# Per-row statistics of the quantised weights, and the removal of the rounding constant together with the zero point, issued on GpSimd instead of VectorE

## The chip, the cores and the metric

The kernel runs on one core of one Trainium2 chip. The metric is device time in microseconds of one execution. The kernel before took 2467.56, 2470.31 and 2482.42 us in three runs; the median is 2470.31 us. In the profile's rows PE is TensorE (matrix products), PEld its weight loads, DVE is VectorE, ACT is ScalarE, POOL is GpSimd, SP is the engine that issues most transfers. The clock is the share of full speed that the throttle granted TensorE.

## What is computed

Four layers follow one another on `x`, two sequences of 1024 tokens with 288 channels, with `ctx`, two sequences of 154 tokens, as context. Attention has 16 heads of 18 channels. Layers 0 and 1 are quantised blocks, layers 2 and 3 plain attention from `x` to `ctx`, whose keys are taken as two sets (86 and 68), each with a softmax of its own. What the change concerns is the quantised product in layers 0 and 1:

```python
def quant_linear(q, s, qsum, w, b):
    wmax = jnp.max(w, axis=1)
    wmin = jnp.min(w, axis=1)
    sw = (wmax - wmin) / 255.0 + 1e-08
    zw = _ste_round(-wmin / sw) - 128.0
    qw = jnp.clip(_ste_round(w / sw[:, None]) + zw[:, None], -128.0, 127.0)
    acc = jnp.einsum('bnk,ok->bno', q, qw) - qsum * zw
    return acc * (s * sw) + b
...
h = layer_norm(x, ln1_g, ln1_b, 1e-06)
q8, s, sm = quant_act(h)
q = quant_linear(q8, s, sm, wq1, bq1).reshape(b, n, H, D)
k = quant_linear(q8, s, sm, wk1, bk1).reshape(b, n, H, D)
v = quant_linear(q8, s, sm, wv1, bv1).reshape(b, n, H, D)
a = attn(q, k, v)
a8, sa, sma = quant_act(a)
x = x + quant_linear(a8, sa, sma, wo1, bo1)
...
h = quant_linear(q8, s, sm, wfc1, bfc1)
```

After the self-attention come a cross-attention to `ctx` with a mask (`wq2` and `wo2` quantised, `wk2` and `wv2` not) and a feed-forward 288 to 1152 to 288 with a gelu (`wfc1`, `wfc2` quantised). `_ste_round` rounds to the nearest integer, ties to even.

## The kernel before

**Weights.** Every quantised weight is loaded, quantised row by row with its output channels on the partitions, transposed on TensorE and kept. `quantise_rows` (from L218) does the quantising. It is called by `prep` (L305: wv1, wo1, wo2 and four blocks of 288 rows of wfc1, on 96 partitions in three slices of 288), by `prep_T` (L322: wk1, wq1, wq2, on 108 partitions in three slices of 288) and by `prep_fc2` (L337: wfc2 in three blocks of 96 rows, each one slice of 1152). A layer has 13 such weights, layers 0 and 1 together 26.

**One weight.** The steps of `quantise_rows`, all on VectorE unless another engine is named: L225 and L226 take the maximum and minimum of each row (three per partition, or one for wfc2). L227 and L228 make the scale `sw`, L229 its reciprocal `rs`, L231 and L232 the largest magnitude in units of the scale, L233 the rounding constant `mg` (the constant whose addition rounds a float to an integer, or 0 where the values are so large that nothing is to be rounded), L234 to L237 the zero point `zw`. Then, for each slice of 288 or 1152, L240 multiplies by `rs` and adds `mg`, which rounds, and L243 takes `mg` off again and adds `zw`. L248, on GpSimd, clips the whole weight from both sides and writes it as bf16. GpSimd then makes the twelve extra columns that carry zero point and bias through the product (L253 to L261, with the helper `three`, L210 to L216, which splits a number into three parts). The transposes on TensorE wait for the clipped weight and these columns.

**Buffers.** The float weight stands in a tile of pool `big` (three buffers), the clipped one in `bf` (three), the statistics in `wstat` (two).

**Order.** Every engine works its own queue in order. A planner with a time model (L57, `tc.block(schedule_with_timeline_sim=True)`) sets the order in the queues, so that instructions of several stages are interleaved. The main line is the self-attention: for each of two layers and two sequences it makes logits on TensorE twice, once with the queries on the partitions (L600), whose rows VectorE reduces to their maxima (L607, 1024 instructions), and once the other way (L660), whose exponentials ScalarE makes (L662); L674 multiplies them by the values. The logits go through three banks of PSUM (pool `ps_s`, L68), which both kinds share. `beside` (L1623) feeds pieces of a side line between the pieces of the main one. The prologue prepares layer 0's wk1, wq1 and wv1 (`prepare_first`, from L997). Then stand, beside the four self-attentions: layer 0's wo1 and the second sequence's queries and keys, wq2 and wo2, fc1 and fc2; then the rest of layer 0's block for the first sequence, with layer 1's wk1, wq1, wv1; then layer 1's wo1 and the rest for the second sequence, with layer 1's wq2 and wo2; last layer 1's fc1 and fc2. Layers 2 and 3 follow without quantised weights.

**Other work on GpSimd** that the prediction names: the mask's addition to the logits of the cross-attention (L641), the layer norm's power (L414, small; L416 on VectorE takes it up) and its gain and offset (L430), additions to the residual (L472), the splitting of queries and keys into bf16 parts (L510, L517), and the transfers issued there (L178, L200, L1402). L646 on VectorE takes the maxima of the cross-attention's logits after L641.

Of the kernel before, what the change touches and what calls it, by code (L numbers as in the profile page):

```python
# [13 lines left out]
ALU = mybir.AluOpType  # L14
# [3 lines left out]
B, S, C, T = 2, 1024, 288, 154  # L18
# [13 lines left out]
MAGIC = 12582912.0  # L32
# [12 lines left out]
NZ = 12  # L45
# [8 lines left out]
def tile_xattn(ctx: ExitStack, tc: tile.TileContext, ins: dict, out: bass.AP):  # L54
    nc = tc.nc
# [86 lines left out]
    def bf(name):  # L142
        return work.tile([P, 3 * HQ], BF16, tag="bf", name=name, bufs=3)
# [71 lines left out]
        eng.tensor_tensor(r, r, high, ALU.subtract)  # L215
        eng.tensor_tensor(low, r, middle, ALU.subtract)  # L216

    def quantise_rows(w, bias, n, width, pad, name):  # L218

        rows = w.shape[0]
        wm = small.tile([rows, 10, 3], F32, tag="wstat", name=name, bufs=2)
        mx, mn, sw, rs, am, mg, u, zw, z, be = (wm[:, j, 0:n] for j in range(10))
        nc.vector.tensor_reduce(mx, w, AX.X, ALU.max)  # L225
        nc.vector.tensor_reduce(mn, w, AX.X, ALU.min)  # L226
        nc.vector.tensor_tensor(sw, mx, mn, ALU.subtract)  # L227
        nc.vector.tensor_scalar(sw, sw, 1.0 / 255.0, 1e-8, ALU.mult, ALU.add)  # L228
        nc.vector.reciprocal(rs, sw)  # L229

        nc.vector.scalar_tensor_tensor(am, mn, -1.0, mx, ALU.mult, ALU.max)  # L231
        nc.vector.tensor_tensor(am, am, rs, ALU.mult)  # L232
        nc.vector.tensor_scalar(mg, am, 4194304.0, MAGIC, ALU.is_lt, ALU.mult)  # L233
        nc.vector.tensor_tensor(u, mn, rs, ALU.mult)  # L234
        nc.vector.scalar_tensor_tensor(u, u, -1.0, mg, ALU.mult, ALU.add)
        nc.vector.tensor_tensor(u, u, mg, ALU.subtract)
        nc.vector.tensor_scalar(zw, u, 128.0, None, ALU.subtract)  # L237
        for j in range(n):
            c = slice(j, j + 1)
            nc.vector.tensor_scalar(  # L240
                w[:, j, :], w[:, j, :], rs[:, c], mg[:, c], ALU.mult, ALU.add
            )
            nc.vector.tensor_scalar(  # L243
                w[:, j, :], w[:, j, :], mg[:, c], zw[:, c], ALU.subtract, ALU.add
            )
        q = bf(f"{name}q")
        qv = view(q[:rows, 0 : n * (width + pad)], n=n, i=width + pad)
        nc.gpsimd.tensor_scalar(qv[:, :, 0:width], w, 127.0, -128.0, ALU.min, ALU.max)  # L248

        def col(k):  # L250
            return qv[:, :, width + k]

        nc.gpsimd.tensor_copy(z, zw)  # L253
        three(nc.gpsimd, [col(2 * k) for k in range(3)], z)
        nc.gpsimd.tensor_copy(
            qv[:, :, width + 1 : width + 6 : 2], qv[:, :, width : width + 6 : 2]
        )
        nc.gpsimd.tensor_tensor(be, bias, rs, ALU.mult)
        three(nc.gpsimd, [col(6), col(7), col(9)], be)
        for k, src in ((8, 6), (10, 7), (11, 6)):  # L260
            nc.gpsimd.tensor_copy(col(k), col(src))  # L261
        if pad > NZ:
            nc.gpsimd.memset(qv[:, :, width + NZ :], 0.0)
        return qv, sw
# [54 lines left out]
        scale_row(row, [sw[:, n : n + 1] for n in range(3)], name)  # L319
        return qw, row  # L320

    def prep_T(W, w_name, b_name, scaled=False, queue=nc.sync, bias=None):  # L322


        name = w_name
        col = W.tile([FR, 3], F32, "col", f"{name}col")
        if bias is None:
            bias = bias_cols(b_name, [(f, f + FR) for f in FT], f"{name}b")
        wv = view(big(f"{name}w")[:FR, 0 : 3 * C], n=3, i=C)
        for n, f in enumerate(FT):  # L330
            queue.dma_start(out=wv[:, n, :], in_=ins[w_name][f : f + FR, :])
        qv, sw = quantise_rows(wv, bias, 3, C, NZ, f"{name}s")
        qw = transpose_weight(W, qv, FR, name)
        nc.vector.tensor_scalar(col, sw, SCALE if scaled else 1.0, None, ALU.mult)
        return qw, col
# [618 lines left out]
    class SelfAttention:  # L954
# [42 lines left out]
        def prepare_first(self):  # L997

            w, b, name = self.w, self.b, self.name
            self.begin()
            w["ln"] = load_ln(WA, L0, 1)
            scales, qs = [], []

            def tile():
                t = query_tile(f"{name}f", "qTb")
                return t.rearrange("p j t -> p (j t)")[:, 0 : 3 * HQ]

            def normalise(hf):  # L1010
                h = apool.tile([P, HC, C], F32, tag="a", name=f"{name}h", bufs=2)
                s = small.tile([P, HC], F32, tag="st", name=f"{name}st")
                c0 = b * 8 + hf * HC
                q = ln_quantise(
                    c0, w["ln"], 1e-6, s, f"{name}l", h, tile(), nc.vector
                )
                scales.append(s)
                qs.append(q)

            def linear(hf, part, rows):  # L1020
                return linear_T(
                    qTs[hf], w[part], sbs[hf], rows[hf], f"{name}{part}", nc.vector
                )

            def scale_tile():
                return work.tile([P, HQ], F32, tag="e", name=f"{name}sb", bufs=8)[:FR]

            names = [(f"{L0}w{part}1", f"{L0}b{part}1") for part in "kqv"]
            biases = [
                bias_cols(col, [(f, f + FR) for f in FT], f"{col}t", nc.scalar)  # L1030
                for _, col in names[:2]
            ]
            load_tokens(0, 2 * HC)
            normalise(0)
            w["k"] = prep_T(WA, *names[0], queue=nc.scalar, bias=biases[0])
            qTs = [transposed(qs[0], f"{name}t", tile())]
            sbs = [token_scales(scales[0], f"{name}sb", scale_tile())]
            normalise(1)
            w["q"] = prep_T(WA, *names[1], scaled=True, queue=nc.scalar, bias=biases[1])
            made = [linear(0, "k", self.k), linear(0, "q", self.q)]  # L1040
            for m in made:
                next(m)
            qTs.append(transposed(qs[1], f"{name}t", tile()))
            sbs.append(token_scales(scales[1], f"{name}sb", scale_tile()))
            made.append(linear(1, "k", self.k))
            next(made[2])

            def others():
                for k in (0, 2, 1):
                    for put in made[k]:  # L1050
                        yield 2
                last_tokens.append(load_tokens(2 * HC, NCH, put))
                w["v"] = prep(WA, *names[2])
                yield 8
                for hf in range(2):
                    self.values(hf, qTs[hf], scales[hf])
                    yield 3
                for put in linear(1, "q", self.q):
                    yield 2

            return others()
# [587 lines left out]
    with tc.tile_pool(name="apool", bufs=1) as apool:  # L1649
        WA, WO = Weights(tpool, 1, 3, 1), Weights(apool, 1, 1, 1)  # L1650
# [97 lines left out]
```

## Time and profile before

The profiled execution spans 2474.0 us from its first to its last instruction; the runs took 2467.56 to 2482.42 us. Its mean granted clock is 0.866.

| stretch (us) | what runs in it | PE | VectorE | ScalarE | GpSimd | clock |
|---|---|---|---|---|---|---|
| 160-220 | attention of layer 0, no weight begins | 56.59 of 60 | 55.82 | 44.13 | 23.57 | 1.00 |
| 220-345 | fc1 and fc2 of layer 0, seven weights | 115.84 of 125 | 118.66 | 85.00 | 37.91 | 0.97 |
| 560-660 | layer 1's wk1, wv1, wq1 | 80.05 of 100 | 90.36 | 50.77 | 30.53 | 0.85 |
| 1240-1480 | fc1 and fc2 of layer 1, seven weights | 184.10 of 240 | 166.94 | 133.51 | 106.30 | 0.79 |

The columns are busy microseconds of each engine in a stretch. Busy time says how full an engine is there, not that others wait for it; a stretch in which one engine is full and the rest are not is paced by that engine. A row of the trace that begins with a time gives start and length of an instruction, then engine, line, operation, what is written and read, the shape, and how many instructions the row stands for. A group's row gives the least, median and largest duration in ns.

The weights start (first L225) at 21.9, 26.1, 44.5, 46.4, 122.4, 145.8 us, then, in layer 0's feed-forward, at 222.3, 253.2, 275.5, 280.7, 303.6, 310.7 and 323.3. Those of layer 1 start at 560.1, 562.0, 642.8, about 775, 1039.3, 1042.2, 1247.6, 1250.1, 1359.6, 1366.1, 1387.3, 1392.4 and 1399.7.

### The profile page before, as it was taken

The numbers are of one execution on the slowest core, as the hardware profiler recorded it, in microseconds if no ns is written. First come the engines' busy times: TensorE is split into PE (matmuls) and PEld (weight loads), VectorE is DVE, ScalarE is ACT, GpSimd is POOL, SyncE is SP. The second block draws the span as 40 slices with busy tenths as digits, with TensorE's granted clock in tenths as the row PEclk, the third lists the DMA queues.
The fourth block names the chain that finished last, engine by engine and source line by source line (L and its number), as shares of the span: only waits on it lengthen the run. The fifth ranks groups of instructions, "written<-read, shape, count | busy, mean of one in ns | idle before, by whom it ended". The sixth has DMA issues, their size and how long they took to land. (4 is left out here: it accounts for less than half of the span.)

```text
span 2474.0 us, 33572 instructions
## 1 busy us (share of the span) xinstructions
PE 1950.8 (79%) x10524; PEld 847.7 (34%) x10524; DVE 1772.7 (72%) x4213; ACT 1476.1 (60%) x2897; POOL 972.2 (39%) x2038
## 2 busy tenths in 40 slices
PE   2579988788776878887679668887778886788887
PEld 1223333332233243323333233333334343443443
DVE  6699987699775658997559848893345686656665
ACT  3257767676477667756766257756646564554443
POOL 4334224651325455532353545523157462423210
PEclk9689999899787979998889589986877888889998
DMA  3523212221001322110032031100122311212221
GB/s 75 168 66 100 68 35 69 70 64 33 13 7 47 113 71 64 44 29 14 6 100 85 23 86 43 46 9 12 31 76 87 89 48 28 55 51 81 81 66 37
DMA packets 160003, 141.58 MB, mean 57 GB/s; under 512 B 44123, under 2 KB 156339, under 8 KB 159760
## 3 DMA queue, kind: packets, MB, share of 16 engines
q1 hardware_dynamic: 148656, 121.90, 17.0%
q0 software_dynamic: 3584, 12.04, 2.0%
q10 hardware_dynamic: 7584, 5.47, 1.2%
q8 instruction: 84, 1.38, 0.2%
q14 instruction: 95, 0.78, 0.1%
HBM read 96.60 MB, written 39.37 MB: 55 GB/s over the span
## 5 line engine op out<-in xcount | busy, mean ns | idle before, releaser
L662 ACT ACTIVATE L_xattn_aatse<-L_xattn_aats 128x512 f32<-128x512 f32 x1024 | 576.3, 597 | 277.1 <-PE L_xattn_aats L660 267.2
L607 DVE TENSOR_REDUCE L_xattn_amxh<-L_xattn_amx 128x1 f32<-128x512 f32 x1024 | 658.4, 679 | 74.5 <-PE L_xattn_amx L600 71.9
L660 PE MATMUL L_xattn_aats<-L_xattn_aqT,kT 120*128 120x512 bf16 x1024 | 392.2, 409 | 88.0 <-ACT L_xattn_aatse L662 46.2
L600 PE MATMUL L_xattn_amx<-kT,L_xattn_aqT 108*128 108x512 bf16 x1024 | 387.9, 414 | 65.1 <-DVE L_xattn_amxh L607 39.5
L674 PE MATMUL L_xattn_aato<-L_xattn_aatse,L_xattn_av 128*32 128x512 f32 x2048 | 300.9, 660 | 43.7 <-ACT L_xattn_aatse L662 40.6
L641 POOL TENSOR_TENSOR L_xattn_bmxm<-L_xattn_bmxm,L_xattn_bm 128x308 f32<-128x308 f32 x256 | 200.0, 787 | 158.4 <-ACT L_xattn_bmxm L640 150.4
L660 PEld LDWEIGHTS <-kT 120*128 120x128 bf16 x1024 | 96.7, 101 | 336.2 <-issue 298.7
L662 ACT ACTIVATE L_xattn_atse<-L_xattn_ats 86x512 f32<-86x512 f32 (+1 forms) x256 | 142.7, 590 | 95.0 <-PE L_xattn_ats L660 82.2
L600 PEld LDWEIGHTS <-L_xattn_aqT 108*128 108x128 bf16 x1024 | 102.7, 103 | 216.7 <-issue 162.5
L646 DVE TENSOR_REDUCE L_xattn_mxn<-L_xattn_mx 128x2 f32<-128x172 f32 (+1 forms) x512 | 124.8, 303 | 30.7 <-PE L_xattn_mx L630 27.4
L640 ACT COPY L_xattn_bmxm<-L_xattn_bmx 128x308 f32<-128x308 f32 x256 | 104.1, 417 | 67.9 <-PE L_xattn_bmx L630 23.7
L646 DVE TENSOR_REDUCE L_xattn_bmxn<-L_xattn_bmxm 128x2 f32<-128x308 f32 x256 | 116.8, 461 | 30.6 <-POOL L_xattn_bmxm L641 30.3
L660 PE MATMUL L_xattn_ats<-L_xattn_qT,L_xattn_kT 120*86 120x512 bf16 (+1 forms) x256 | 99.7, 422 | 40.8 <-DMA L_xattn_qT<-L_xattn_mxsr 18.6
L746 DVE TENSOR_TENSOR L_xattn_batse<-L_xattn_bats,L_xattn_bmT 128x512 f32<-128x512 f32 x160 | 107.5, 680 | 25.7 <-PE L_xattn_bats L752 7.5
L747 ACT ACTIVATE L_xattn_batse<-L_xattn_batse 128x512 f32<-128x512 f32 x160 | 100.3, 631 | 40.6 <-DVE L_xattn_batse L746 36.4
L1494 PE MATMUL L_xattn_o<-wo,L_xattn_p 128*128 128x288 f32 x320 | 99.9, 451 | 5.5 <-DVE L_xattn_p L819 4.6
L674 PEld LDWEIGHTS L_xattn_aato<-L_xattn_aatse,L_xattn_av 128*32 128x32 f32 x2048 | 42.2, 112 | 173.2 <-ACT L_xattn_aatse L662 144.1
L847 DVE STREAM_TRANSPOSE L_xattn_atT<-L_xattn_ato 128x512 f32<-128x512 f32 x64 | 45.6, 713 | 61.6 <-PE L_xattn_ato L674 50.1
L630 PE MATMUL L_xattn_mx<-L_xattn_kT,L_xattn_qT 108*128 108x154 bf16 x512 | 68.9, 250 | 24.1 <-DMA L_xattn_qT<-L_xattn_r 10.4
L630 PE MATMUL L_xattn_bmx<-L_xattn_bkT,L_xattn_bqT 108*128 108x154 bf16 x512 | 72.0, 244 | 16.1 <-ACT L_xattn_bmxm L640 7.1
L1360 PE MATMUL L_xattn_co<-L_xattn_wfc2t,L_xattn_cgT 117*128 117x288 bf16 x320 | 62.4, 346 | 23.4 <-ACT L_xattn_cgT L1357 22.4
L674 PE MATMUL L_xattn_ato<-L_xattn_atse,L_xattn_v 68*32 68x512 f32 (+1 forms) x512 | 74.9, 649 | 6.7 <-ACT L_xattn_atse L662 5.8
(632 smaller groups left out, 3782.0 us busy)
## 6 DMA issues: line engine op xcount, KB each, us to landing
kT<-L_xattn_akr SPq DMA_DIRECT2D x192, 72.0 KB
L_xattn_aqT<-L_xattn_aqr SPq DMA_DIRECT2D x192, 72.0 KB
L_xattn_bqT<-L_xattn_bqr SPq DMA_DIRECT2D x192, 72.0 KB
L_xattn_qT<-L_xattn_r SPq DMA_DIRECT2D x192, 72.0 KB
L_xattn_akr<-L_xattn_akst SPq DMA_DIRECT2D x16, 324.0 KB
L_xattn_aqr<-L_xattn_aqst SPq DMA_DIRECT2D x16, 324.0 KB
L_xattn_bqr<-L_xattn_bqst SPq DMA_DIRECT2D x16, 324.0 KB
L_xattn_r<-L_xattn_qst SPq DMA_DIRECT2D x16, 324.0 KB
```

Of the source, the lines that this page charges most:

```text
L600: nc.tensor.matmul(sp, lhsT=qt[:KR, j, c * P : (c + 1) * P], rhs=kt[:KR, j, a * 512 : (a + 1) * 512], start=True, stop=True,)
L607: nc.vector.tensor_reduce(halves[:, a, c, j, :], sp, AX.X, ALU.max, negate=True)
L630: nc.tensor.matmul(sp[:, j * T : (j + 1) * T], lhsT=qt[:KR, 2 * a + j, c * P : (c + 1) * P], rhs=kt[:KR, 4 * g + 2 * a + j, 0:T], start=Tr ...
L640: nc.scalar.copy(lm, of)
L641: nc.gpsimd.tensor_tensor(lm, lm, mask[:, c : c + 1, 0:T].to_broadcast([P, 2, T]), ALU.add)
L646: nc.vector.tensor_reduce(nm[:, c, 2 * a : 2 * a + 2, n], of[:, :, k0:k1], AX.X, ALU.max, negate=True,)
L660: nc.tensor.matmul(sp, lhsT=keys(j), rhs=qt[:KM, j, :], start=True, stop=True)
L662: nc.scalar.activation(e, sp, AF.Exp)
L674: made = nc.tensor.matmul(po[32 * i : 32 * i + 32, :], lhsT=lhsT, rhs=rhs, start=start, stop=stop)
L746: nc.vector.tensor_tensor(e, sp, maskT[:, m, :], ALU.add)
L747: nc.scalar.activation(e, e, AF.Exp)
L1494: nc.tensor.matmul(ps, lhsT=t[:, c * P : (c + 1) * P], rhs=wo[:, u0 + u, :], start=(u == 0), stop=(u == len(tiles) - 1),)
```

## The change

The statistics `sw` (two instructions), the product for the largest magnitude, `mg`, the product with the minimum, and the steps to `zw` go to an engine that is handed in, by default GpSimd; so does a new small instruction, `u = zw - mg`. The second instruction of every slice becomes `w + u` with an upper bound of 127, on that engine, in place of `w - mg + zw` on VectorE. The clip (L248, on GpSimd as before) keeps only the lower bound. The reductions, the reciprocal, L231 and the first instruction of every slice (L240) stay on VectorE. Layer 0's wk1 and wq1, in the prologue, hand in VectorE.

```diff
--- before.py
+++ after.py
@@ -215,7 +215,7 @@
         eng.tensor_tensor(r, r, high, ALU.subtract)
         eng.tensor_tensor(low, r, middle, ALU.subtract)
 
-    def quantise_rows(w, bias, n, width, pad, name):
+    def quantise_rows(w, bias, n, width, pad, name, eng=nc.gpsimd):
 
 
 
@@ -224,28 +224,29 @@
         mx, mn, sw, rs, am, mg, u, zw, z, be = (wm[:, j, 0:n] for j in range(10))
         nc.vector.tensor_reduce(mx, w, AX.X, ALU.max)
         nc.vector.tensor_reduce(mn, w, AX.X, ALU.min)
-        nc.vector.tensor_tensor(sw, mx, mn, ALU.subtract)
-        nc.vector.tensor_scalar(sw, sw, 1.0 / 255.0, 1e-8, ALU.mult, ALU.add)
+        eng.tensor_tensor(sw, mx, mn, ALU.subtract)
+        eng.tensor_scalar(sw, sw, 1.0 / 255.0, 1e-8, ALU.mult, ALU.add)
         nc.vector.reciprocal(rs, sw)
 
         nc.vector.scalar_tensor_tensor(am, mn, -1.0, mx, ALU.mult, ALU.max)
-        nc.vector.tensor_tensor(am, am, rs, ALU.mult)
-        nc.vector.tensor_scalar(mg, am, 4194304.0, MAGIC, ALU.is_lt, ALU.mult)
-        nc.vector.tensor_tensor(u, mn, rs, ALU.mult)
-        nc.vector.scalar_tensor_tensor(u, u, -1.0, mg, ALU.mult, ALU.add)
-        nc.vector.tensor_tensor(u, u, mg, ALU.subtract)
-        nc.vector.tensor_scalar(zw, u, 128.0, None, ALU.subtract)
+        eng.tensor_tensor(am, am, rs, ALU.mult)
+        eng.tensor_scalar(mg, am, 4194304.0, MAGIC, ALU.is_lt, ALU.mult)
+        eng.tensor_tensor(u, mn, rs, ALU.mult)
+        eng.tensor_tensor(u, mg, u, ALU.subtract)
+        eng.tensor_tensor(u, u, mg, ALU.subtract)
+        eng.tensor_scalar(zw, u, 128.0, None, ALU.subtract)
+        eng.tensor_tensor(u, zw, mg, ALU.subtract)
         for j in range(n):
             c = slice(j, j + 1)
             nc.vector.tensor_scalar(
                 w[:, j, :], w[:, j, :], rs[:, c], mg[:, c], ALU.mult, ALU.add
             )
-            nc.vector.tensor_scalar(
-                w[:, j, :], w[:, j, :], mg[:, c], zw[:, c], ALU.subtract, ALU.add
+            eng.tensor_scalar(
+                w[:, j, :], w[:, j, :], u[:, c], 127.0, ALU.add, ALU.min
             )
         q = bf(f"{name}q")
         qv = view(q[:rows, 0 : n * (width + pad)], n=n, i=width + pad)
-        nc.gpsimd.tensor_scalar(qv[:, :, 0:width], w, 127.0, -128.0, ALU.min, ALU.max)
+        nc.gpsimd.tensor_scalar(qv[:, :, 0:width], w, -128.0, None, ALU.max)
 
         def col(k):
             return qv[:, :, width + k]
@@ -319,7 +320,7 @@
         scale_row(row, [sw[:, n : n + 1] for n in range(3)], name)
         return qw, row
 
-    def prep_T(W, w_name, b_name, scaled=False, queue=nc.sync, bias=None):
+    def prep_T(W, w_name, b_name, scaled=False, queue=nc.sync, bias=None, eng=nc.gpsimd):
 
 
         name = w_name
@@ -329,7 +330,7 @@
         wv = view(big(f"{name}w")[:FR, 0 : 3 * C], n=3, i=C)
         for n, f in enumerate(FT):
             queue.dma_start(out=wv[:, n, :], in_=ins[w_name][f : f + FR, :])
-        qv, sw = quantise_rows(wv, bias, 3, C, NZ, f"{name}s")
+        qv, sw = quantise_rows(wv, bias, 3, C, NZ, f"{name}s", eng)
         qw = transpose_weight(W, qv, FR, name)
         nc.vector.tensor_scalar(col, sw, SCALE if scaled else 1.0, None, ALU.mult)
         return qw, col
@@ -1032,11 +1033,15 @@
             ]
             load_tokens(0, 2 * HC)
             normalise(0)
-            w["k"] = prep_T(WA, *names[0], queue=nc.scalar, bias=biases[0])
+            w["k"] = prep_T(
+                WA, *names[0], queue=nc.scalar, bias=biases[0], eng=nc.vector
+            )
             qTs = [transposed(qs[0], f"{name}t", tile())]
             sbs = [token_scales(scales[0], f"{name}sb", scale_tile())]
             normalise(1)
-            w["q"] = prep_T(WA, *names[1], scaled=True, queue=nc.scalar, bias=biases[1])
+            w["q"] = prep_T(
+                WA, *names[1], scaled=True, queue=nc.scalar, bias=biases[1], eng=nc.vector
+            )
             made = [linear(0, "k", self.k), linear(0, "q", self.q)]
             for m in made:
                 next(m)
```

## The prediction

> **What bounds the kernel now.** The page came first: shares and slices.
>
> ```profile
> PE 1950.8 (79%) x10524; PEld 847.7 (34%) x10524; DVE 1772.7 (72%) x4213; ACT 1476.1 (60%) x2897; POOL 972.2 (39%) x2038
> ...
> DVE  6699987699775658997559848893345686656665
> ...
> POOL 4334224651325455532353545523157462423210
> ```
>
> TensorE is the busiest engine, but VectorE (DVE) stands at 9 in nine of the 40 slices, while GpSimd (POOL) never passes 7. The chain of waits was read next. Its pieces start at 1975.80 us and the last weight is finished at about 1430, so it says nothing of the stages this change touches. Those have to be read by stretches, cut where the page of line L225 (first instruction of every weight) puts the weights.
>
> ```profile
> core 0: us, PE busy (x) PEld busy (x) DVE busy (x) ACT busy (x) POOL busy (x), PEclk, DMA share, GB/s
> 260.00:300.00 40.00, 37.71 (x231) 13.13 (x231) 39.66 (x101) 27.94 (x53) 10.35 (x47) 1.00 0.23 61
> 560.00:620.00 60.00, 50.09 (x254) 15.46 (x254) 57.54 (x130) 35.67 (x69) 9.41 (x33) 0.96 0.14 39
> 1360.00:1410.00 50.00, 31.58 (x117) 12.89 (x116) 49.62 (x121) 12.39 (x24) 23.43 (x73) 0.53 0.08 20
> 1700.00:1900.00 200.00, 155.68 (x785) 74.46 (x786) 84.23 (x229) 115.61 (x232) 82.48 (x155) 0.77 0.21 56
> ```
>
> The columns are busy time and, in brackets, instructions of TensorE, its weight loads, VectorE, ScalarE and GpSimd, then the granted clock. In 260-300 and 560-620, which hold weights, VectorE works 39.66 of 40 and 57.54 of 60 us (the same view gives 79.40 of 80 for 1030-1110). In 1360-1410 it works 49.62 of 50 and the granted clock has fallen to 0.53. In 1700-1900, which has no weight, it works 84 of 200. GpSimd has between half and five sixths of each stretch free. Which wait ends last there, in 220-345 where seven weights lie:
>
> ```profile
> ACT L_xattn_aatse L662 <- PE L_xattn_aats L660: 34.0, 38, 2.6
> ...
> DVE L_xattn_amxh L607 <- PE L_xattn_amx L600: 4.6, 8, 2.0
> ```
>
> VectorE waited 4.6 of 125 us for TensorE's logits; ScalarE waited 34.0 us for TensorE, which was itself behind the logits that VectorE had not yet reduced. So VectorE's queue sets the pace where weights are prepared, and TensorE follows closely (37.71 of 40 busy in 260-300). It has room: in 150-175 it fed 36 reductions of line L607 in 25 us with 22.99 us busy, in 275-300 only 23.
>
> **The change part by part.** 26 weights are quantised, 13 to a layer; two stay, so 24 change: 18 of three slices of 288 and 6 (fc2) of one slice of 1152.
>
> *Removed from VectorE.* Per weight eight small instructions (L227, L228, L232 to L237) and the slices of L243. What they cost a full queue is the distance from start to start, not the listed duration:
>
> ```profile
> 1369.85 0.15 DVE L227 TENSOR_TENSOR L_xattn_wfc_864s<-L_xattn_wfc_864s 96x3 f32<-96x3 f32 x1
> 1369.92 0.17 DVE L231 SCALAR_TENSOR_TENSOR L_xattn_wfc_864s<-L_xattn_wfc_864s 96x3 f32<-96x3 f32 x1
> ...
> 1377.87 1.09 DVE L243 TENSOR_SCALAR L_xattn_wfc_576w<-L_xattn_wfc_576w,L_xattn_wfc_576s 96x288 f32<-96x288 f32 x3
> 1378.89 1.68 DVE L240 TENSOR_SCALAR L_xattn_wfc_864w<-L_xattn_wfc_864w,L_xattn_wfc_864s 96x288 f32<-96x288 f32 x3
> ...
> 1406.43 4.76 DVE L243 TENSOR_SCALAR L_xattn_wfc2w<-L_xattn_wfc2w,L_xattn_wfc2s 96x1152 f32<-96x1152 f32 x1
> ```
>
> The two small ones start 0.07 us apart, and the next three follow at 1370.02, 1370.09 and 1370.17, so 0.08 each: 8 x 0.08 x 24 = 15.4 us. By their durations (0.15) it would be 28.8. Three slices of L243 take 1.02 us from 1377.87 to 1378.89 (18 x 1.02 = 18.4); the slice of 1152 takes 0.79 (from 1395.10 to 1395.89; 6 x 0.79 = 4.7). Together 38.5 us, by durations 53.8 (1.10 and 0.87). The rows of the removed lines also hold about 17 us of stretching (0.1 to 3.9 us in some twenty instructions, the last row above the worst) while GpSimd worked. I count none of it, because the instruction next in VectorE's queue would wait in its place; 17 more is the end of the range.
>
> *Added to VectorE.* One small instruction in each of the two prologue weights: 2 x 0.15 = 0.3 us.
>
> *Added to GpSimd.* Nine small instructions a weight and the slices. Its own small ones (L253, L258 on 96x3) last 0.19 us: 24 x 9 x 0.19 = 41 us. A slice is priced from the same operation with two immediates:
>
> ```profile
> L248 POOL TENSOR_SCALAR L_xattn_wfc_0sq<-L_xattn_wfc_0w x2: 902/902/903, 245.3 to 1337.2; 96x864 bf16<-96x864 f32 x2
> ...
> L248 POOL TENSOR_SCALAR L_xattn_wfc2s1q<-L_xattn_wfc2w x2: 1142/1142/1142, 335.5 to 1399.8; 96x1152 bf16<-96x1152 f32 x2
> ```
>
> (1142 - 902) / 288 = 0.83 ns an element, so 288 elements are 0.42 us: 18 x 3 x 0.42 + 6 x 1.14 = 30 us. An operand for each row is not shown by any row; the dearer end is the two-input 128x288 addition of L430 (0.80 us), which makes the slices 62 us. The pass of L248 loses one of its two operations; one pass of the same length, I leave it at its price. GpSimd thus goes from 972 to 1043 us (1075 at the dear end), and the cover is its idle time: 30 of 40 us in 260-300, 51 of 60 in 560-620. Queued behind the new work are the splits of maxima (L213 to L216), L430, L472, L510, L517 and the loads that GpSimd issues (L200, L178, L1402).
>
> The Trainium skill (GPSIMD Engine Reference, section 4.1) advises against this: elementwise work belongs on VectorE, GpSimd being about twice as slow on two inputs and near line rate on one. The rows agree on slices, but put a small instruction at 0.19 against 0.15, not twice; by the factor of two GpSimd would add 65 us instead of 41, still inside its idle time.
>
> *New waits.* VectorE now waits twice in each weight: L229 for the scale, L240 for the magic constant. Behind either stand the reductions of L607, and behind those TensorE, which has three banks for logits. Two rows show VectorE taking something back from GpSimd:
>
> ```profile
> L646 DVE TENSOR_REDUCE L_xattn_bmxn<-L_xattn_bmxm 128x2 f32<-128x308 f32 x256 | 116.8, 461 | 30.6 <-POOL L_xattn_bmxm L641 30.3
> ```
>
> 30.3 us over 256 hand-overs is 0.12; line L416 behind the small L414 waits 5.2 us over 24, or 0.22, and is the nearer (small instructions both ways). 48 x 0.22 = 11 us. The ends are 0 (a planner sets the order and may fill the gap with L607) and the 0.79 of one addition standing ahead, 38 us.
>
> *Two engines on one weight.* The slices of GpSimd now run beside VectorE's own L240 of the same weight. What that may cost shows where VectorE's slices met other work of GpSimd: L240 at 1378.89 met an L248 that ran from 1379.06 to 1380.08, and the last L243 met L430:
>
> ```profile
> 1407.54 3.04 POOL L430 TENSOR_TENSOR L_xattn_blh<-L_xattn_blh,L_xattn_ln 128x288 f32<-128x288 f32 x4
> ```
>
> Three slices took 1.68 instead of 1.10 us at 1378.89; the 1152 slice took 4.76 instead of 0.87 until four additions had ended. From nothing (VectorE's slices follow one another at 0.34 us and GpSimd comes after) to 2 x 0.42 x 18 = 15 us. I take a third, 5 us, since most slices (414 to 428 ns) show no stretching.
>
> The skill (SBUF — State Buffer, "SBUF: two separate sides") says that GpSimd and a VectorE instruction that uses both port pairs exclude one another for a whole instruction, whoever starts first. Taken strictly, every slice pair collides and the 5 become 15 us; the 4.76 row, which outlasted several GpSimd instructions, is even worse than that.
>
> *Sum.* -38.5 + 0.3 + 11 + 5 = -22 us of VectorE time. Of the 24 weights 21 lie where VectorE is full; L1's wo1 (775-800, 17.92 of 25) and two fc1 blocks (1250-1275, 20.07 of 25) do not: 22 x 21 / 24 = -19 us. Next in line is TensorE. The profiled execution spans 2474.0 us, among the runs' 2467.56 to 2482.42 and 3.7 above their median; nothing around the span is listed. 2470 - 19 = **2451 us**; as the profile has it, 2455.
>
> **The rivals.** *Slower: the hand-overs cost more than the work.* Place: VectorE's queue at L229 and L240, above all in 1387-1420, where three fc2 weights follow one another and GpSimd runs L430 of the next stage back to back, and at 625-637 (L430 and L472, 0.79 each). There GpSimd, at about 3 us of new work a weight, can become the one waited for. It decides at 38.5 / 48 = 0.8 us a hand-over: one addition ahead of each breaks even, two (1.58) give 76 - 38 = +38, or about 2508. Against it: all of VectorE's waits for GpSimd listed today are some 68 us, and most weights have spare time before their use (wq2's L243 ends at 135.6, its L248 starts at 200.55).
>
> *Nothing lands.* TensorE, at 94% in 260-300, is as close as it looks, or the planner rearranges the queues and spends it elsewhere: 2462 to 2475. Against it: the 36 reductions per 25 us above.
>
> *More lands.* The 17 us of stretching go too, and durations rather than distances count: -54 - 17 + 16 = -55, about 2415. For it: the clock is 0.53 in 1360-1410 because TensorE starves (31.58 of 50 busy). Against: the next instruction inherits such waits.
>
> That the change moves nothing is excluded by the diff: every named call changes its engine.
>
> **How the numbers follow.** A measurement of this kernel tells 1% from no change, some 25 us (2446 and 2495). The forecast has 0.52. Its own range is 2425 to 2462: at the good end durations and the cheaper waits (-53.8 + 0.3 + 6 + 2 = -45), at the bad end distances, 0.31 a hand-over and every slice pair colliding (-38.5 + 0.3 + 15 + 15 = -8). The 1% line cuts this range, 0.27 beyond and 0.25 within. Nothing lands has 0.16, all within; more lands 0.07, all faster; slower 0.25, of which 0.20 beyond 1%. That is 0.34 faster, 0.46 same, 0.20 slower. The range 2424 to 2492 leaves out most of "more" and the upper half of "slower".
>
> **What would show it.** VectorE busy down by about 50 us, GpSimd up by 70 (110 at most); a slice on GpSimd 0.42 us and a small one 0.19; more reductions of L607 per 25 us between 220 and 345 and after 560; the end of layer 0's last fc2 weight 10 us earlier. Wrong if VectorE shows waits for GpSimd at the reciprocal or at L240 of more than 0.8 us each, if L240's mean rises well over 0.5 us, or if 1375-1475 grows longer.

## The result, and the profile after

The changed kernel takes 2484.21 us (median of 13 runs, 2476.99 to 2496.95), the kernel before in the same comparison 2470.22 us (13 runs). The ratio is 1.0061, 95% interval 1.0044 to 1.0078: 0.6% slower, where 0.8% faster was the forecast's centre. The time lies inside the outer range of 2424 to 2492 us, but outside the forecast's own 2425 to 2462, and the change went the other way. The profiled execution spans 2482.4 us (before 2474.0).

The page of the changed kernel, the same three places as before (TensorE, VectorE, GpSimd; busy time, then forty slices in tenths):

```profile
PE 1938.0 (78%) x10524; PEld 843.1 (34%) x10524; DVE 1748.8 (70%) x3963; ACT 1469.9 (59%) x2893; POOL 1140.6 (46%) x2314
...
DVE  6699986689774767998459848993345676656665
...
POOL 6445654644526464652363955513157462423310
```

VectorE lost 24 us, not 50. GpSimd gained 168 us, not 70, and stands at 9 in the slice from 1365 to 1427 us. The stretches of the changed kernel, same columns as before:

```profile
core 0: us, PE busy (x) PEld busy (x) DVE busy (x) ACT busy (x) POOL busy (x), PEclk, DMA share, GB/s
260.00:300.00 40.00, 38.27 (x228) 13.00 (x226) 36.81 (x73) 27.90 (x53) 27.53 (x78) 1.00 0.22 54
560.00:620.00 60.00, 52.98 (x294) 17.55 (x290) 57.72 (x118) 38.58 (x73) 26.38 (x65) 1.00 0.12 30
1360.00:1410.00 50.00, 37.06 (x165) 14.39 (x161) 44.28 (x86) 15.39 (x30) 40.73 (x108) 0.66 0.10 29
```

The stretches lie at the same times as before, so the work in them is only roughly the same. In 260-300 the relief that was forecast is there (VectorE 36.81 instead of 39.66), in 560-620 it is not (57.72 instead of 57.54). In 1360-1410 GpSimd now works 40.73 of 50 us. Why, the lines of the slices (L244) and of the clip (L249) show; the three numbers are the shortest, median and longest duration in ns:

```profile
L244 POOL TENSOR_SCALAR L_xattn_wfc_576w<-L_xattn_wfc_576w,L_xattn_wfc_576s x6: 1241/1256/1577, 285.5 to 1376.5; 96x288 f32<-96x288 f32 x6
...
L244 POOL TENSOR_SCALAR L_xattn_wfc2w<-L_xattn_wfc2w,L_xattn_wfc2s x6: 4193/4206/4211, 316.7 to 1431.2; 96x1152 f32<-96x1152 f32 x6
...
L249 POOL TENSOR_SCALAR L_xattn_wfc_0sq<-L_xattn_wfc_0w x2: 2371/2388/2405, 247.6 to 1343.4; 96x864 bf16<-96x864 f32 x2
```

A slice takes 1.25 us on 288 elements and 4.2 on 1152, where the forecast had 0.42 and 1.14. The clip, which lost one of its two operations, went from 0.90 up to 2.4 us. Summed over the trace, slices are 93.7 us, the clip is 40.4 us dearer, and the 216 small instructions, with a mean of 0.24 us, are 51 us.

### The profile page after: what moved, and what is told of

It is laid out like the page before. It is cut to its first block, busy times and chain, and to the rows that moved or that the text cites. A ratio compares the mean times of both kernels' runs of the same rounds, so it can differ in the third digit from the quotient of the medians.

```text
span 2482.4 us, 33589 instructions
## 1 busy us (share of the span) xinstructions
PE 1938.0 (78%) x10524; PEld 843.1 (34%) x10524; DVE 1748.8 (70%) x3963; ACT 1469.9 (59%) x2893; POOL 1140.6 (46%) x2314
## 5 line engine op out<-in xcount | busy, mean ns | idle before, releaser
L608 DVE TENSOR_REDUCE L_xattn_amxh<-L_xattn_amx 128x1 f32<-128x512 f32 x1024 | 655.7, 679 | 80.2 <-PE L_xattn_amx L601 77.5
L675 PE MATMUL L_xattn_aato<-L_xattn_aatse,L_xattn_av 128*32 128x512 f32 x2048 | 294.1, 648 | 42.8 <-ACT L_xattn_aatse L663 40.5
L601 PEld LDWEIGHTS <-L_xattn_aqT 108*128 108x128 bf16 x1024 | 102.7, 103 | 204.9 <-issue 146.6
L675 PEld LDWEIGHTS L_xattn_aato<-L_xattn_aatse,L_xattn_av 128*32 128x32 f32 x2048 | 42.4, 111 | 171.0 <-ACT L_xattn_aatse L663 144.9
```

Of the source, the lines that this page charges most:

```text
L601: nc.tensor.matmul(sp, lhsT=qt[:KR, j, c * P : (c + 1) * P], rhs=kt[:KR, j, a * 512 : (a + 1) * 512], start=True, stop=True,)
L608: nc.vector.tensor_reduce(halves[:, a, c, j, :], sp, AX.X, ALU.max, negate=True)
L675: made = nc.tensor.matmul(po[32 * i : 32 * i + 32, :], lhsT=lhsT, rhs=rhs, start=start, stop=stop)
```

## What the longer instructions do to VectorE

Two costs show up on VectorE. The first is in its list of waits; columns are the waiting line, the line it waited for, total us, times, longest. Before:

```profile
DVE L_xattn_aqy L552 <- POOL L_xattn_akst L517: 1.5, 2, 1.0
DVE L_xattn_aky L552 <- POOL L_xattn_akst L517: 1.4, 2, 1.1
```

After (these lines are one higher):

```profile
DVE L_xattn_aqy L553 <- POOL L_xattn_akst L518: 18.9, 3, 7.4
...
DVE L_xattn_aky L553 <- POOL L_xattn_aqst L518: 7.9, 3, 3.9
...
DVE L_xattn_wfc2s L229 <- POOL L_xattn_wfc2s L228: 4.4, 1, 4.4
```

All waits of VectorE for GpSimd add up to 68.3 us before and 100.3 after. Hardly any of that is at the new hand-overs: the reciprocal (L229) waits once, 4.4 us, and L241 shows no wait (in two of the three other orders below L241 waits too, 3.7 us). Of the 32.0 us, 30.0 are at L553 (33.7 after, 3.7 before), for the splitting of queries and keys (L511 and L518), which had been in GpSimd's queue all along and now stands behind slices. The longest of these waits, VectorE's row first, then what GpSimd did meanwhile:

```profile
1270.57 0.75 DVE L553 SCALAR_TENSOR_TENSOR L_xattn_aqy<-L_xattn_aq,L_xattn_wq1col,L_xattn_asb 108x512 f32<-108x512 f32 x1 [7.36 <-POOL L_xattn_akst L518]
```

```profile
1260.90 3.72 POOL L244 TENSOR_SCALAR L_xattn_wfc_0w<-L_xattn_wfc_0w,L_xattn_wfc_0s 96x288 f32<-96x288 f32 x3
1264.60 3.69 POOL L244 TENSOR_SCALAR L_xattn_wfc_288w<-L_xattn_wfc_288w,L_xattn_wfc_288s 96x288 f32<-96x288 f32 x3
1268.26 1.16 POOL L511 TENSOR_TENSOR L_xattn_aqy<-L_xattn_aqy,L_xattn_aqst 108x512 f32<-108x512 f32 x1
1269.38 1.15 POOL L518 TENSOR_TENSOR L_xattn_akst<-L_xattn_aky,L_xattn_akst 108x512 bf16<-108x512 f32 x1
```

VectorE was idle from 1263.21 to 1270.57, and the slices cost the same 1.24 us each beside it. So their price does not come from VectorE working beside them.

The second cost does not appear as a wait, since a held instruction counts as busy. Around 1414 us in the changed kernel, VectorE's row first, then GpSimd's:

```profile
1414.13 3.88 DVE L375 TENSOR_SCALAR L_xattn_bst<-L_xattn_blqs 128x4 f32<-128x4 f32 x1
```

```profile
1413.80 4.19 POOL L244 TENSOR_SCALAR L_xattn_wfc2w<-L_xattn_wfc2w,L_xattn_wfc2s 96x1152 f32<-96x1152 f32 x1
```

L375 works on four elements a row and usually takes 0.16 us. Here it ends at 1418.01, with GpSimd's slice at 1417.99. Summed over all lines of VectorE that the change does not move, durations rise by 28.8 us in this trace (L386 by 11.7, L231 and L375 by 7.4 each). Not all of this is new: about 17 us of such stretching stood in the removed lines before, and may only have moved on. Counting every VectorE instruction that lasts over 0.15 us longer than the median of its kind, the excess is 44.8 us before and 55.5 after, and each of them overlaps work of GpSimd; beside the slices and the clip it is 18.6 us, beside the clip before 3.6.

What is left over for VectorE has to be read from its busy time, which counts overlapping instructions once. The moved instructions had taken 73.6 us by their durations, but these overlap, and others grew longer: busy time fell by 23.9 us (1772.7 to 1748.8), and the waits for GpSimd rose by 32.0. So nothing is left over in this order; together VectorE's work and these waits grew by 8 us.

TensorE meets the price most plainly at the last weight of all:

```profile
1438.76 1.03 PE L357 MATMUL L_xattn_wfc2pt<-ident,L_xattn_wfc2s2q 96*117 96x96 bf16 x8 [11.27 <-POOL L_xattn_wfc2s2q L249]
```

It was idle for 11.27 us until GpSimd's clip of that weight was through.

## Experiments: the price of an instruction on GpSimd

Each experiment stands with its edit; ratios are against the kernel before, run on the same chip in the same comparison.

The first run leaves the four layers out and has GpSimd go through twelve forms, among them:

```diff
+for _ in range(reps): g.tensor_scalar(W, W, u, 127.0, ALU.add, ALU.min)           # L80
+for _ in range(reps): g.tensor_scalar(W, W, 0.5, 127.0, ALU.add, ALU.min)         # L86
+for _ in range(reps): g.tensor_scalar(W, W, 127.0, -128.0, ALU.min, ALU.max)      # L88
+for _ in range(reps): g.tensor_scalar(W, W, -128.0, None, ALU.max)                # L90
+for _ in range(reps): g.tensor_tensor(W, W, u.to_broadcast([rows, n]), ALU.add)   # L92
```

> Leaves the four layers out: x is copied to the output, and GpSimd runs twelve forms of elementwise instruction one after another on 96 partitions, first alone on 288 and on 1152 elements, then on 288 with VectorE running 400 slices of the form of L240 beside it. If operand kind sets the price: a per-row column with an immediate 1.25 us on 288 and 4.2 on 1152 (as in the changed kernel), two immediates about 0.4 and 1.1, one immediate with no second operation about 0.85 and 3.1. If instead the price in the changed kernel came from contention with VectorE, the column form alone takes about 0.42 us and rises to 1.25 only beside VectorE. If VectorE's slices are held up by GpSimd, their durations rise from 0.42 us beside it, for some forms more than for others.

VectorE's slices (L111, the form of L240) began at once and ran beside nearly all of it, so no phase shows GpSimd alone; its prices agreed in all phases, and the slices beside an idle VectorE above took 1.24 us too. The groups of GpSimd in its last phase; the columns are count, busy us, mean ns, idle before:

```profile
L80 POOL TENSOR_SCALAR w<-w,st 96x288 f32<-96x288 f32 x8 | 10.2, 1271 | 0.8
...
L90 POOL TENSOR_SCALAR w<-w 96x288 f32<-96x288 f32 x8 | 7.4, 922 | 0.7
...
L92 POOL TENSOR_TENSOR w<-w,st 96x288 f32<-96x288 f32 x8 | 5.3, 662 | 0.6
L88 POOL TENSOR_SCALAR w<-w 96x288 f32<-96x288 f32 x8 | 3.4, 424 | 0.7
```

The dear one is the operation, not the operand: addition and minimum cost 1.27 us with a column and 1.20 with two immediates (L86), while minimum and maximum with two immediates cost 0.42. One operation alone (0.92) is dearer than that pair. The output type changes nothing (0.42 and 0.92 in bf16 as well). An addition with the column broadcast as a second input costs 0.66, half of the form that the change uses; on 1152 elements it is 2.10 against 4.16.

The same run shows the holding. VectorE's slice beside GpSimd's 1152-element column form, and at the end, when GpSimd was idle:

```profile
L111 DVE TENSOR_SCALAR e<-d,sd x4: 515/4330/4340, 76.3 to 85.3; 96x288 f32<-96x288 f32 x4
...
L111 DVE TENSOR_SCALAR e<-d,sd x9: 409/414/416, 295.9 to 298.7; 96x288 f32<-96x288 f32 x9
```

A slice of 0.41 us lasts 4.33, as long as the instruction beside it. Beside the short forms (0.42, 0.66 and 0.79 us) exactly one slice gets through per GpSimd instruction; beside the 288-element column form the pace was 0.45 us a slice, three in each of GpSimd's 1.27 us.

## Experiments: which part of the change costs

Both bounds in the clip again:

```diff
-nc.gpsimd.tensor_scalar(qv[:, :, 0:width], w, -128.0, None, ALU.max)
+nc.gpsimd.tensor_scalar(qv[:, :, 0:width], w, 127.0, -128.0, ALU.min, ALU.max)
```

> The changed kernel with both bounds in the clip again (the upper one is then applied twice). Theory 1, GpSimd's prices make the weights late: L249 goes back to 0.90 and 1.14 us, GpSimd's busy time from 1141 to about 1102 us, and the time falls by 4 to 10 us, to 2474 to 2480. Theory 2, what counts is VectorE held up by the slices on GpSimd: L386, L375 and L231 stay stretched (30 us together over before) and the time stays at 2480 to 2488. Theory 3, what counts is the new order of instructions: the time moves either way by as much, with no relation to the 39 us.

1.0062 (1.0037 to 1.0086). GpSimd falls to 1103.3 us, as expected, and the time does not follow; VectorE's unmoved lines stay 35.8 us longer than before. The reverse, the clip with one operation in the kernel before:

```diff
-nc.gpsimd.tensor_scalar(qv[:, :, 0:width], w, 127.0, -128.0, ALU.min, ALU.max)
+nc.gpsimd.tensor_scalar(qv[:, :, 0:width], w, -128.0, None, ALU.max)
```

> The kernel before with the upper bound of the clip left out, so that L248 has one operation; no value is then held to 127. It adds 18 x 1.47 + 8 x 1.98, some 40 us, to GpSimd and nothing else. Theory 1: 4 to 10 us slower than before (2474 to 2480), TensorE's transposes waiting for the clip. Theory 2: no change beyond 3 us, since VectorE's own work stays. Theory 3 (order): a change of either sign of up to 10 us.

1.0010 (0.9983 to 1.0037). At this setting the 40 us of the clip do not decide the time, added or taken away, which speaks against theory 1 as far as the clip goes.

Only the statistics moved (slices as before on VectorE, both bounds in the clip):

```diff
-eng.tensor_scalar(w[:, j, :], w[:, j, :], u[:, c], 127.0, ALU.add, ALU.min)
+nc.vector.tensor_scalar(w[:, j, :], w[:, j, :], mg[:, c], zw[:, c], ALU.subtract, ALU.add)
```

> The changed kernel with the slices as before on VectorE (w - mg + zw) and both bounds in the clip; only the small statistics stay on GpSimd, with one small instruction (u) that nothing reads. Theory 1 (GpSimd's prices): GpSimd about 1025 us, the time at or below before, 2455 to 2470, since only small instructions are added. Theory 2 (VectorE held up by the slices): the stretch of L386, L375 and L231 goes too, the same 2455 to 2470. Hand-overs as the cause: it stays at 2480 or above, since all of the reciprocals and first slices still wait for GpSimd. Theory 3 (order): anywhere from 2460 to 2490.

0.9999 (0.9977 to 1.0021). In this order no cost of the hand-overs shows, though all of them are there, and eight small instructions less on VectorE bring nothing either. Only the slices moved (statistics on VectorE, both bounds):

```diff
-eng.tensor_tensor(sw, mx, mn, ALU.subtract)
+nc.vector.tensor_tensor(sw, mx, mn, ALU.subtract)
...
+nc.vector.tensor_tensor(u, zw, mg, ALU.subtract)
```

> The statistics back on VectorE (with the one new small instruction u there), only the slices on GpSimd, both bounds in the clip. If the slices on GpSimd (1.27 us on 288, 4.2 on 1152, about 94 us in all) are the cause: 1.005 to 1.010, the same as with the statistics moved, or a little worse since VectorE has the small instructions again. If the hand-overs at the reciprocal and at L240 add to it: at or below 1.003.

1.0133 (1.0107 to 1.0159), worse than with the statistics moved as well: in this order, the loss sits with the slices. How they cost so much here is not shown: VectorE's unmoved lines are only 16.6 us longer than before, its waits for GpSimd 8.1 us longer and its busy time 1.6 us less, some 6 us in all against 33 measured.

The slices in the cheaper form, both bounds in the clip:

```diff
-eng.tensor_scalar(w[:, j, :], w[:, j, :], u[:, c], 127.0, ALU.add, ALU.min)
+eng.tensor_tensor(w[:, j, :], w[:, j, :], u[:, c].to_broadcast([rows, width]), ALU.add)
```

> The changed kernel with both bounds in the clip, and the slices on GpSimd as an addition of a broadcast column: 0.66 us on 288 and 2.10 on 1152 instead of 1.27 and 4.16, so some 48 us instead of 94. If the length of GpSimd's slices sets the loss: half of it, 1.002 to 1.004. If it is VectorE being held (a slice beside this form took 0.73 us from start to start, against 0.47 beside the other): no better, 1.005 or more. If it is that the weight's path crosses engines once more, whatever the length: no better either, but then VectorE's L386, L375 and L231 are not stretched.

0.9887 (0.9860 to 0.9913): 2442.61 us against 2468.09, faster than both kernels. Its slices in the trace:

```profile
L244 POOL TENSOR_TENSOR L_xattn_wfc2w<-L_xattn_wfc2w,L_xattn_wfc2s x6: 2099/2102/2102, 311.0 to 1394.9; 96x1152 f32<-96x1152 f32 x6
```

GpSimd's slices are 49.5 us instead of 93.7, and VectorE's unmoved lines only 18.3 us longer than before (in the two other orders of the next section 35.7 and 12.0, so this sum follows the order as well). The same form twice, so that the slices take as long as in the changed kernel:

```diff
+eng.tensor_tensor(w[:, j, :], w[:, j, :], mg[:, c].to_broadcast([rows, width]), ALU.subtract)
+eng.tensor_tensor(w[:, j, :], w[:, j, :], zw[:, c].to_broadcast([rows, width]), ALU.add)
```

> The slices on GpSimd as two additions of broadcast columns (minus mg, then plus zw), 2 x 0.66 us on 288 and 2 x 2.10 on 1152: as long in all as the column form of the changed kernel (1.27 and 4.16), each instruction half of it. Length of the weight's path on GpSimd as the cause: the gain of the single addition (0.989) is gone, 1.003 to 1.009. The instruction's form as the cause (VectorE held for the whole of one long instruction of 4.2 us): at most half of the gain is gone, 0.990 to 0.996. A chance order of instructions as the cause of the gain: anything from 0.99 to 1.01.

1.0080 (1.0050 to 1.0110). In this one order the gain is gone, as the length of the path would have it and not the form; VectorE's unmoved lines are 34.2 us longer than before. The cheap form with the statistics on VectorE, by the edit already shown:

> The slices on GpSimd as one addition of a broadcast column (0.66 and 2.10 us), the statistics on VectorE. If the two parts add up (statistics worth 0.7% where the slices are on GpSimd, by 1.0133 against 1.0062): 0.994 to 0.998. If the statistics' gain was order alone: 0.987 to 0.991, as with both.

0.9995 (0.9974 to 1.0015). In this order of instructions the statistics are worth 1.1% beside cheap slices, 0.7% beside dear ones and nothing beside slices on VectorE; the next section says how far one order can be trusted.

GpSimd kept busy with work that nothing reads, after each weight of the kernel before:

```diff
+for j in range(4 if aside[0] > 1 else 0):
+    nc.gpsimd.tensor_scalar(spare[:rows], spare[:rows], neghalf[:rows, 0:1], 127.0, ALU.add, ALU.min)
```

> The kernel before with four instructions of the form of the moved slices (column added, then the minimum with 127) on a tile of 192 columns of their own after each weight but the first two: about 24 x 4 x 0.9 = 86 us more on GpSimd, which nothing reads. GpSimd's occupation as the cause (its queue and VectorE held by it): 1.004 to 1.008, as in the changed kernel. The longer path of each weight as the cause: within 0.3% of 1.

1.0037 (1.0013 to 1.0060), between the two expectations. GpSimd rose to 1057.9 us, VectorE's unmoved lines by 9.9 us, and its waits for GpSimd did not rise (65.0 us). The 0.4% is no more than a new order alone can make (next section), so this run decides neither way; also the pieces were only 192 elements wide, in bf16, and nobody waited for them.

## Experiments: how much is the order of the instructions

The planner makes a new order for every edit. To see what that alone does, the spacing of the side lines was changed a little: their pieces are spread over the main line's 128 steps so that the last is fed by step 112, here by step 111:

```diff
-beside(main, 128, side, n, 112)
+beside(main, 128, side, n, 111)
```

This edit, with 111, 110 or 113, was made in the kernel before, the changed kernel, the kernel with both bounds in the clip and the one with broadcast additions, as far as the table below is filled:

> The kernel before with the side lines fed by the 111th instead of the 112th step of the main line: no instruction is added, removed or moved to another engine, only the order in the queues changes (thousands of rows). It says how much a new order alone is worth. Order as the cause of the 0.6%: a ratio beyond 1.004 or below 0.996. The slices as the cause: within 0.3% of 1.

> The kernel with single additions of a broadcast column, with the side lines fed by the 111th step instead of the 112th: the same instructions in another order. If the gain belongs to the instructions: 0.986 to 0.993. If it was a lucky order: back to 0.997 or above.

> The changed kernel with both bounds in the clip and the side lines fed by the 111th step: the same instructions as the earlier run with both bounds, in another order. If the loss belongs to the instructions: 1.003 to 1.009. If it was an unlucky order: 0.999 or below.

> The kernel before with the side lines fed by the 110th step: another order of the same instructions. It goes with the next run. If orders scatter by half a per cent: 0.995 to 1.005.

> The changed kernel, side lines fed by the 110th step. If the 0.6% belongs to the instructions moved: 0.4 to 0.9% above the run before it (before_110). If it belongs to the order that the planner happened to make: between 0.5% below and 0.3% above it.

> The kernel before with the side lines fed by the 113th step. If orders scatter by half a per cent: 0.995 to 1.005.

> The changed kernel, side lines fed by the 113th step. If the 0.6% belongs to the instructions moved: 0.4 to 0.9% above before_113. If it belongs to the order: between 0.5% below and 0.3% above it.

> The changed kernel, side lines fed by the 111th step, the fourth pair; the kernel before at that setting stood at 1.0021 (0.9996 to 1.0046). If the instructions cost 0.6%: 1.006 to 1.011. If the loss is the order's: 0.998 to 1.006.

> Single additions of a broadcast column (0.66 and 2.10 us a slice), both bounds in the clip, side lines fed by the 110th step; the kernel before stood there at 0.9999 and the changed one at 1.0019. If shorter slices are worth something in every order: 0.990 to 0.997. If the 0.9887 was a lucky order alone: 0.998 or above.

All ratios against the kernel before at its own setting, 112:

| setting | kernel before | changed | column form, both bounds | broadcast addition, both bounds |
|---|---|---|---|---|
| 112 | 1 | 1.0061 (1.0044-1.0078) | 1.0062 (1.0037-1.0086) | 0.9887 (0.9860-0.9913) |
| 111 | 1.0021 (0.9996-1.0046) | 1.0064 (1.0042-1.0085) | 1.0015 (0.9994-1.0035) | 0.9985 (0.9965-1.0005) |
| 110 | 0.9999 (0.9974-1.0023) | 1.0019 (0.9996-1.0042) | | 0.9938 (0.9919-0.9957) |
| 113 | 1.0059 (1.0035-1.0082) | 1.0014 (0.9996-1.0032) | | |

The kernel before scatters over 0.6% by its order alone, the broadcast form over 1.0%. Changed less before at the same setting is +0.61, +0.43, +0.20 and -0.45%: a mean of +0.20%, with 0.23% of standard error from the four. So the loss of 0.6% is measured at the setting that the kernel has, but it cannot be put down to the moved instructions as such; their own share is between a small gain and a small loss. The expectations split in the same way: the changed kernel at 111 and the broadcast form at 110 came out where the instructions were to be the cause, the changed kernel at 110 and 113 and the broadcast form at 111 where the order was; the column form with both bounds fell between, the kernel before stayed within 0.3% at 111, as if the order cost nothing, and scattered more than expected at 113.

The broadcast form is below the kernel before in all three pairs (-1.13, -0.36, -0.61; mean -0.70%, standard error 0.23%) and below the changed one in all three (-1.74, -0.79, -0.81; mean -1.11%). Against the column form with the same clip it is -1.75 and -0.30% in two pairs. Three orders are few, and at 111 its interval reaches 1, but all three lie below all four of the kernel before (0.9999 at the least) and below all six with the column form (1.0014 at the least). So shorter slices are worth something, and how much is known roughly.

Averaging over the orders also shows where the time goes. I took the times at which certain of the 1024 reductions (L607, L608) end, one profile for each setting, as mean and extremes in us:

| stretch, by the kernel before | before, 4 orders | changed, 4 orders | broadcast, 3 orders |
|---|---|---|---|
| start to first reduction (78) | 78.2 (76.4-79.4) | 82.5 (80.7-83.5) | 80.2 (79.0-81.0) |
| 225-383, fc1 and fc2 of layer 0 | 155.6 (152.6-158.2) | 144.7 (143.1-146.6) | 141.3 (140.4-141.8) |
| 383-450, start of the cross-attention | 70.8 (67.2-74.9) | 76.3 (74.2-77.8) | 76.8 (75.0-78.5) |
| 1283-1482, fc1 and fc2 of layer 1 | 202.5 (197.6-209.1) | 202.2 (198.3-206.4) | 192.4 (190.2-195.5) |
| 1660 (last reduction) to the end, no quantised weight | 809.2 (794.5-822.3) | 815.0 (811.1-822.0) | 808.8 (799.6-817.1) |

In 225-383 the main line gains 10.9 us on average, and something in every order, in the place that the forecast named. Half of it (5.5 us) is lost in the next 67 us on average, in the changed and in the broadcast form alike, though at setting 111 the changed kernel loses none of it (74.2 against 74.9). A likely reason, not tested, is that the main line there meets a chain (attention output, projection, layer norm, queries) that had not become earlier: in the changed kernel at 112 the transposes of layer 0's last fc2 weight start at 355.3 us, 3 us later than before, although the reductions then run 5 to 7 us earlier. The start loses 4.3 us. In 1283-1482, where three fc2 weights follow one another, the changed kernel gains nothing on average and loses 6.6 us at setting 112 (206.4 against 199.8); the broadcast form gains 10 us.

Up to the last reduction, which holds all the weights, the changed kernel is 3.3 us shorter on average and the broadcast form 23.5. The rest differs without any weight: at 112 the broadcast form's profiled execution is 42.4 us shorter than the one before, and 14.3 us of that come after the last reduction. Nor is all of it order: at 112 and 113 the kernel before starts the same instructions in the same order on every engine there, and takes 813.9 and 822.3 us. These are single executions.

## Why the prediction was wrong, step by step

**The bound** held where the forecast had read it: with VectorE relieved, the stretch 225-383 ran 7% shorter on average, and shorter in all four orders.

**Removed from VectorE** held in what was taken away: 73.6 us by durations, against 53.8 and some 17 of stretching. That stretching would only move on fits the trace too, and some more came (below). With collisions, the forecast's terms give 38.5 - 0.3 - 5 = 33 us less work for VectorE; its busy time fell by 23.9.

**Added to GpSimd** is the step that failed: "a slice is priced from the same operation with two immediates". It was not the same operation. L248's pair of minimum and maximum is the one cheap pair among the forms measured (0.42 us); addition and minimum are 1.27. The 30 us were 93.7, beyond the end taken as dear (62). The extrapolation itself was right for L248's own form (0.42 us measured on 288 elements); what was not asked is whether another pair of operations costs the same. Likewise "one pass of the same length, I leave it at its price": the clip went from 0.90 to 2.4 us, 40 us in all. That part of the miss cost nothing at setting 112 (1.0061 with one bound, 1.0062 with both) and 0.5% at 111 (1.0064 and 1.0015), within what the order does.

**New waits** is the term in which, by the traces, most of the wrong price reached VectorE: 11 us forecast, 32.0 measured. With the broadcast form's shorter slices the rise is 17.0, 14.4 and 1.6 us at settings 112, 111 and 110, against 32.0, 31.7 and 12.6. At the hand-overs it was not too low: 4.4 us at the reciprocal and none at L241 in this order, 4.4 to 8.5 in the four. What stands behind GpSimd's new work was listed (the splits of L510 and L517 among it) and not priced: 30.0 of the 32 us are at L553 for L518.

**Two engines on one weight**, 5 us with an end of 15, came out near the dear end: 38.5 - 0.3 - 23.9 = 14 us by busy time. The 28.8 us of longer durations, less some 17 that may only have moved on, give 12. It was not at the place named. L241, the slices of the same weight, did not stretch (mean 0.49 us, before 0.51); the short instructions of the activations did (L375, L386), and L231. The Trainium skill (SBUF — State Buffer, "SBUF: two separate sides"), that GpSimd and a VectorE instruction on both port pairs exclude one another for a whole instruction, was the better guide here: 3.88 us for four elements, and 4.33 us for a slice beside a 1152-element instruction. Whether these two use both port pairs no run shows. Beside the 288-element column form the measurement differs from it, with three slices let through per instruction. The skill's other rule (GPSIMD Engine Reference, section 4.1), near line rate on one input, does not hold for the form used: 1.27 us on one input and a column, where VectorE's slice takes 0.41, and 0.66 with the column broadcast as a second input.

**Sum.** Forecast were 22 us less of VectorE's time. Measured, busy time and waits for GpSimd together give -23.9 + 32.0 = +8 us at setting 112, where the time rose by 14. Over the four orders the means are -23.2 and +27.9, or +5 us, and the time gave +0.20%, some 5 us, with as much uncertainty. That the means agree is partly luck, since single pairs are off by up to 16 us. For the broadcast form the same account over three orders gives -34.1 + 11.0 = -23 us, and the time -0.70%, some 17 us. The forecast's -19 us is thus about what the change is worth when GpSimd's slices cost what the forecast's range for them allowed (49.5 us between 30 and 62) and the clip keeps its price.

**The rivals.** The slower one had one right place (three fc2 weights in succession, where TensorE waits 11.27 us for the clip) and the wrong mechanism: 4.4 us over 48 hand-overs at L229 and L240 are 0.09 each, not 0.8. Of the signs, those of size missed: VectorE's busy time fell by 24 us and not 50, GpSimd's rose by 168 and not 110 at most, a slice took 1.25 us, and layer 0's last fc2 weight came 3 us later and not 10 earlier. The signs of error came only in part: one long wait (4.4 us) at the reciprocal, no stretched L240, and a longer 1283-1482 at setting 112 but not on average. The cost went mostly to places that the forecast had not priced. One effect was named under "nothing lands" but never sized: a new order of the same instructions moves this kernel by up to 0.6%, three quarters of the forecast gain.

What stays open: why one order is 0.6 or 1% better than another, why slices alone on GpSimd cost 1.3% in theirs, why the start lost 4.3 us, how the loss divides between waiting and holding, and how much of 0.9887 is the order's.

## What to carry to other kernels

Price an instruction on GpSimd by its exact pair of operations, not by its shape: on 288 elements the forms ranged from 0.42 to 1.47 us, and leaving out one operation made one twice as dear. Before moving work to an engine with idle time, list the old work in its queue that others wait for, and the short instructions of VectorE that a long one beside them will hold. Where a planner reorders everything at each edit, measure the edit in several orders before believing an effect below one per cent.

## What the runs showed of the hardware that was not expected

On GpSimd, minimum then maximum with two immediates took 0.42 us on 96x288, maximum alone 0.92, two columns (subtract, add) 1.47, addition of a broadcast column 0.66. VectorE's slice (0.41 us alone) took 4.33, 3.27 and 1.30 us beside 1152-element instructions of 4.16, 3.11 and 1.14 us, so it waited out each of them.
